# Attention block with residual on one core: first and last steps reordered on GpSimd and VectorE, and filler products on TensorE at the start

## The chip, the core and the metric

The kernel runs on one core of a Trainium2 chip. A core has five engines, each with its own instruction queue that it works through in order: TensorE (PE in the profile, its weight loads PEld), VectorE (DVE), ScalarE (ACT), GpSimd (POOL) and SyncE (SP, which here only issues DMAs). Engines wait for one another through semaphores. The metric is the device time of one execution in microseconds (us), as a median over runs.

## The reference

One layer of multi-query attention over 64 batches of 128 tokens with 512 features, 16 heads of width 64, added to its input. Cut to what matters:

```python
B, N, DIM, H, DH = 64, 128, 512, 16, 64
xn  = layernorm(x, g_in)                        # (x-mean)*rsqrt(var+1e-5)*g
q   = (xn @ Wq).reshape(B, N, H, DH).transpose(0, 2, 1, 3) * DH**-0.5
k, v = split(xn @ Wkv)                          # one key and value head for all 16
k   = concat([null_kv[0], k]); v = concat([null_kv[1], v])      # one null token
sim = einsum('bhid,bjd->bhij', q, k) + concat([null_attn_bias, attn_bias])
sim = where(causal, -max, sim); sim = where(mask, sim, -max)
out = einsum('bhij,bjd->bhid', softmax(sim), v)
x   = x + layernorm(out.reshape(B, N, H*DH) @ Wo, g_out)
```

All of it is fp32.

## The kernel before

**Tiles and stages.** Tokens are taken in rows of 128 (`m`), four rows to a group (`g`), 16 groups; a batch `b` is 128 tokens. For each batch the scores of all 16 heads, `S[b]`, lie in one SBUF tile of 128 x 16 x 129, of which column 128 is the null token. Three such tiles rotate (pool `sp`, three buffers, which the start also uses for `prod`). `S[b]` is first filled with bias plus mask (`bias_mask`, L370, POOL) and with the null column (L376, POOL). The scores are then added from PSUM in two halves of eight heads (L396, DVE), each followed by its negative maximum (L397, DVE). Sixteen exps run on ACT (L409) and leave their sums; the reciprocals come from DVE (L427), and POOL scales the weights by them (L432). DVE transposes 32 x 32 blocks (`blocks_T`, L448), ten DMAs on SP move the blocks into place (`blocks_move`, L459, tile `aTb`), PE multiplies by the values (`values`, L483), ACT copies the result out (L490), PE multiplies by `wo` (`out_mm`, L502). `out_stats` takes mean and variance (L509 to L513, DVE), the power -1/2 on POOL (L514), and centres and scales by `g_out` (L516, DVE). `residual` multiplies by the power on ACT (L530) and adds x on POOL (L531); `store` writes it.

**Token rows.** `norm_stats` (L197 to L201 on DVE, the power on POOL at L202) and `norm_apply` (nmr L214 on DVE, then L215 on ACT) normalise a row. Rows 0 to 7 are transposed on PE (`norm_T`, L224, and the copy L225 on ACT), later ones on DVE and by DMA. `kv_mm` makes key, value and null score (L256, then L264 to L269 on DVE), `k_T` transposes the key (L275, L277).

**Queries.** For group 0 they are plain products (`q_plain`, L294, copies L301). For the other groups one level of Strassen's scheme is used, seven products instead of eight per block (`product`, L337), with sums of the weights made once (`weight_sums`, L304 to L307, DVE, both inputs in SBUF) and sums of the tokens once per group (`token_sum`, L320, POOL). Partial products are copied out on ACT (`keep`, L348) and added on DVE (L355).

**Order.** The order on each engine is written out by hand: what `step(n)` issues first comes first. `step(n)` runs for n from -6 to 62 and works on many batches at once: token row n+10 or n+11 is normalised, keys and values of row n+6 are made, bias and mask of batch n+3 are put down, scores of batch n+2 are made, exps of batch n+1, values of batch n and the output of batch n-1. Steps up to n = 0 are the fill (`fill`), where the halves of the exps are spread out between the query products; from n = 58 on there are no queries left. PSUM is short: products of kv, transposes, values and output (`pw`, `pkv`, `pkT`, `po`, `py`) rotate through two buffers of pool `ps_w`, and the scores through two of `ps_s`.

Lines that set the order around the change:

```python
for m in mns:
    norm_stats(m)
...
if ok(n + 1) and fill:
    exps_half(n + 1, 1)        # exps, reciprocal (DVE), scale (POOL)
...
if ok(n + 2):
    scores(n + 2, 0)
    scores(n + 2, 1)
```

The functions that the diff touches:

Of the kernel before, what the change touches and what calls it, by code (L numbers as in the profile page):

```python
# [8 lines left out]
FP = mybir.dt.float32  # L9
# [8 lines left out]
def kernel(  # L18
# [45 lines left out]
    nc = tc.nc  # L64
# [152 lines left out]
    def norm_T(m):  # L217
        g, t = divmod(m, GB)
        if t == 0:
            xT[g] = gp.tile([P, KC, TOK], FP, tag="xT", name=f"xT_{g}")  # L220
        xh = xs.pop(m)
        pt = ps_w.tile([P, KC, P], FP, tag="w", name=f"pxT_{m}")
        for kc in range(KC):
            nc.tensor.transpose(pt[:, kc, :], xh[:, kc * P : (kc + 1) * P], ident)  # L224
        nc.scalar.copy(xT[g][:, :, t * N : (t + 1) * N], pt)  # L225
# [83 lines left out]
    def token_sum(g, k):  # L309

        xS[g, k] = gp.tile([P, HK, HT], FP, tag=f"xS{k}", name=f"xS{k}_{g}", bufs=1)
        b11, b12 = xT[g][:, lo_k, lo_t], xT[g][:, lo_k, hi_t]
        b21, b22 = xT[g][:, hi_k, lo_t], xT[g][:, hi_k, hi_t]
        p, m = {
            1: (b12, b11),
            2: (b22, xS.get((g, 1))),
            3: (b22, b12),
            4: (b21, xS.get((g, 2))),
        }[k]
        nc.gpsimd.tensor_tensor(xS[g, k], p, m, ALU.subtract)  # L320
# [39 lines left out]
    def mask_neg(g):  # L360
        mneg[g] = gp.tile([P, TOK], FP, tag="mneg", name=f"mneg_{g}")
        nc.vector.tensor_scalar(
            mneg[g], m8s.pop(g), 0.0, NEG, ALU.is_equal, ALU.mult
        )

    def bias_mask(b):
        g, t = divmod(b, GB)
        S[b] = sp.tile([P, 2, NC, N + 1], FP, tag="s", name=f"s_{b}")
        s = S[b].rearrange("p r c j -> p (r c) j")
        nc.gpsimd.tensor_tensor(  # L370
            s[:, :, 0:N],
            bflat,
            mneg[g][:, t * N : (t + 1) * N].unsqueeze(1).broadcast_to([P, H, N]),
            ALU.add,
        )
        nc.gpsimd.tensor_copy(s[:, :, N : N + 1], sn.pop(b).unsqueeze(2))  # L376

    def scores(b, hf):
# [38 lines left out]
    def exps_half(b, hf):  # L417
        exps(b, 8 * hf, 8 * hf + 8)
        rinv(b, hf)
        scale(b, hf)  # L420
# [23 lines left out]
    def blocks_T(b):  # L444

        s = S[b].rearrange("p r c j -> p (r c) j")
        sb = hp.tile([P, NQ, H, Q], FP, tag="sb", name=f"sb_{b}", bufs=1)
        nc.vector.transpose(  # L448
            sb.rearrange("p j h q -> p h j q"),
            s[:, :, 0:N].rearrange("p h (j k) -> p h j k", k=Q),  # L450
        )
        sbs[b] = sb
# [54 lines left out]
    def out_stats(b):  # L507
        st = small.tile([P, 6], FP, tag="st", name=f"sto_{b}")
        nc.vector.bn_stats(st, ys[b])  # L509
        mv = small.tile([P, 2], FP, tag="mvo", name=f"mvo_{b}")  # L510
        nc.vector.bn_aggr(mv, st)
        rstd = small.tile([P, 1], FP, tag="rstdo", name=f"rstdo_{b}")
        nc.vector.tensor_scalar(rstd, mv[:, 1:2], EPS, None, ALU.add)  # L513
        nc.gpsimd.tensor_tensor(rstd, rstd, nhalf, ALU.pow)  # L514
        y = hp.tile([P, DIM], FP, tag="y", name=f"y_{b}")
        nc.vector.scalar_tensor_tensor(  # L516
            y, ys.pop(b), mv[:, 0:1], gob, ALU.subtract, ALU.mult
        )
        if b == B - 1:

            nc.vector.scalar_tensor_tensor(y, y, rstd, res.pop(b), ALU.mult, ALU.add)
        else:
            yr[b] = y, rstd
        ys[b] = y
# [45 lines left out]
    def step(n):  # L570
        def ok(b, end=B):
            return 0 <= b < end

        qg, part = divmod(n + 6, GB)
        mT, mkv, mk = n + 10, n + 6, n + 5
        mns = [m for m in (n + 10, n + 11) if ok(m) and (m >= 2 * GB) == (m == n + 11)]
        if part == 0 and ok(qg + 1, NG) and n + 6 >= 0:
            load_mask(qg + 1)
        q, f = ok(qg, NG), part
        last_g, last_f = divmod(n + 5, GB)  # L580
        fast, last = q and qg > 0, 0 < last_g < NG


        fill = n <= 0
        if fast and f == 0 and fill:
            for k in range(1, 5):
                token_sum(qg, k)
        if ok(n + 3) and q:
            bias_mask(n + 3)
        for m in mns:  # L590
            norm_stats(m)
        if fast and f == 0 and not fill:
            token_sum(qg, 1)

        tT = ok(mT) and mT >= 2 * GB
        if tT and mT % GB:
            tokens_T(mT)
        moves = tT and (mT + 1) % GB == 0
        if moves:
            tokens_move(mT // GB)  # L600
        if ok(n + 1) and not fill:
            exps_half(n + 1, 0)
            exps_half(n + 1, 1)
        if tT and mT % GB == 0:
            tokens_T(mT)
        if ok(n + 3) and not q:
            bias_mask(n + 3)
        if ok(n - 1):
            out_mm(n - 1)
            out_stats(n - 1)  # L610
        if fast and f == 0 and not fill:
            for k in range(2, 5):
                token_sum(qg, k)
        if last:
            product(last_g, last_f, 4, ps_q, "a", start=False)
            q_out(last_g, HC + last_f, lo_t, "a")
            product(last_g, last_f, 3, ps_q, "c", start=False)
            q_out(last_g, last_f, hi_t, "c", "u2")
        if ok(n + 1) and fill:
            exps_half(n + 1, 0)  # L620
        for m in mns:
            norm_apply(m)
        if fast:
            if f == 0:
                qT[qg] = gp.tile([P, NC, TOK], FP, tag="qT", name=f"qT_{qg}")
            product(qg, f, 2, ps_w, "w")
            product(qg, f, 1, ps_q, "a")
            keep("a", "p1")
            q_out(qg, f, lo_t, "w", "p1")
            product(qg, f, 5, ps_q, "c")  # L630
        elif q:
            q_plain(qg, 2 * f)
        if ok(n + 1) and fill:
            exps_half(n + 1, 1)
        if ok(n - 1) and q:
            residual(n - 1)
        if ok(n + 2):
            scores(n + 2, 0)
            if not q and n + 1 < B - 2:
                blocks_T(n + 1)  # L640
            scores(n + 2, 1)
        if n == B - 2:
            attn_T_pe(n)
        if ok(n):
            values(n, 0)
            values(n, 1)
        if ok(n - 1) and not q:
            residual(n - 1)
        if n + 1 in sbs:
            blocks_move(n + 1)  # L650
        if fast:
            product(qg, f, 6, ps_q, "a", start=False)
            keep("a", "u2")
        elif q:
            q_plain(qg, 2 * f + 1)
        if mT < 2 * GB:
            norm_T(mT)
        if ok(mkv) and mkv >= GB - 1:
            kv_mm(mkv)


        if ok(n - 1):
            store(n - 1)
        if not moves:
            loads_late(n)
        if ok(n + 1) and q and not fill:
            blocks_T(n + 1)
            blocks_move(n + 1)
        if moves:
            loads_late(n)  # L670
        if fast:
            product(qg, f, 7, ps_q, "a", start=False)
            keep("a", "u3")
        if ok(mk) and mk >= GB - 2:
            k_T(mk)
        if fast:
            q_out(qg, HC + f, hi_t, "c", "u3")
        if ok(n + 1) and fill:
            blocks_T(n + 1)
            blocks_move(n + 1)  # L680
        if n == -4:
            for m in range(GB - 1):
                kv_mm(m)
                if m:
                    k_T(m - 1)
        if part == 2 and ok(qg, NG):
            mask_neg(qg)


    nc.vector.tensor_scalar(gin8, gin, DH**-0.5, None, ALU.mult)  # L690
# [7 lines left out]
    norm_stats(3)  # L698
    norm_apply(2)
    norm_T(2)  # L700
    norm_apply(3)
    norm_T(3)
    load_second()
    weights_q(2)
    weights_q(0)
# [6 lines left out]
    for n in range(-6, B - 1):  # L712
        step(n)
        if n == -6:
            for kc in range(2):
                weights_kv(kc)
            for kc in range(2, KC):
                weights_kv_prod(kc)
            load_late()
        if n == -5:  # L720
            for kc in range(2, KC):
                weights_kv(kc)
            nc.gpsimd.affine_select(
                bflat,
                bflat,
                pattern=[[0, H], [-1, N]],
                compare_op=ALU.is_ge,
                fill=NEG,
                base=0,
                channel_multiplier=1,  # L730
            )
            weight_sums()

    load_res(B - 1)
# [47 lines left out]
```

## Time and profile before

| | |
|---|---|
| median of 3 runs | 1229.79 us (1229.73 to 1230.2) |
| the profiled execution | 1230.63 us, of which its span, first to last instruction, 1228.5 us |
| TensorE | busy 1183.7 us (96%) |
| VectorE | busy 813.4 us (66%) |
| ScalarE | busy 679.0 us (55%) |
| GpSimd | busy 771.5 us (63%) |
| bias and mask sum, L370 on POOL | 64 of 4535 ns |
| scale, L432 on POOL | 128 of 1900 ns |
| exp, L409 on ACT | 1024 of 392 ns, overlapping with its accumulator read |
| score sum L396 and maximum L397 on DVE | 128 each, 1217 and 1228 ns |
| block transpose L448 on DVE | 62 of 2301 ns |
| mean granted TensorE clock | 0.991 |

A busy share is an average over the whole span. The profile also cuts the span into 40 equal slices of 30.7 us and gives each engine a digit for each (9 is 90% or more), and it lists the time an engine sat idle together with the engine and line whose result ended it. A wait for several semaphores is put down to the one that came last by the profile, which can be a coincidence. A start time and a duration stand ahead of each row of a timeline; the durations on one engine may overlap by about 0.1 us[...].

### The profile page before, as it was taken

How to read it: one execution, taken by the hardware profiler on the slowest of the kernel's cores; microseconds unless marked ns; L12 is line 12 of the kernel's file. 1: busy time of each engine (PE TensorE's matmuls, PEld its weight loads, DVE VectorE, ACT ScalarE, POOL GpSimd, SP SyncE). 2: the span in 40 equal slices, each digit the busy share in tenths (PEclk: the TensorE clock that was granted, in tenths of full speed). 3: DMA queues.
4: the chain of work that ended last, by engine and by line, in shares of the span. 5: the costliest groups of instructions: out<-in, count | busy, mean ns of one | idle time of the engine just before them, and what ended most of it. 6: DMA issues, size and time to landing. Idle time of an engine off the chain costs nothing.

```text
span 1228.5 us, 19153 instructions
## 1 busy us (share of the span) xinstructions
PE 1183.7 (96%) x5968; PEld 750.8 (61%) x5968; DVE 813.4 (66%) x1491; ACT 679.0 (55%) x2563; POOL 771.5 (63%) x520
## 2 busy tenths in 40 slices
PE   5968999999999999999999999999999999999987
PEld 2555666666666666666666666666666666666443
DVE  6565776677677667667767767766776776666652
ACT  3244655665665565566556556556655655554662
POOL 5345747657674765767576585766658576665651
PEclk9979999999999999999999999999999999999999
DMA  6203324333342433334243333434333342322231
GB/s 199 98 14 81 109 78 101 95 101 102 85 113 79 105 96 97 102 83 112 83 106 92 95 100 86 109 85 103 97 89 99 93 105 81 91 70 73 67 88 43
DMA packets 96883, 113.81 MB, mean 93 GB/s; under 512 B 17424, under 2 KB 50704, under 8 KB 96784
## 3 DMA queue, kind: packets, MB, share of 16 engines
q1 hardware_dynamic: 95968, 111.55, 33.2%
q8 instruction: 48, 0.79, 0.3%
q10 hardware_dynamic: 816, 1.05, 0.2%
q14 instruction: 51, 0.42, 0.1%
HBM read 40.45 MB, written 16.78 MB: 47 GB/s over the span
## 4 chain that ended last, share of the span: by engine, by line
PE 87%; ACT 2%; DVE 2%; POOL 2%; issue 1%; SPq 1%; DMA 0%; DVEq 0%; ACTq 0%; POOLq 0%
PE py L502 34%; PE pa L337 17%; PE ps L386 9%; PE po L483 9%; PE pc L337 8%; PE pkv L256 5%; PE pw L337 4%; ACT s L409 2%; POOL s L370 1%; PE pkT L275 1%; SPq L459 0%; DVE s L396 0%; DMA res<-in_x_dram 0%; DVE sb L448 0%; DVE nmax L397 0%
## 5 line engine op out<-in xcount | busy, mean ns | idle before, releaser
L370 POOL TENSOR_TENSOR s<-biasc,mneg 128x2048 f32<-128x2048 f32 x64 | 290.2, 4535 | 332.3 <-DVE sb L448 214.0
L502 PE MATMUL py<-wo,oT 128*128 128x512 f32 x1024 | 453.6, 596 | 5.6 <-ACT oT L490 2.9
L409 ACT ACTIVATE s<-s,nmax 128x129 f32<-128x129 f32 x1024 | 396.2, 392 | 0.0
L502 PEld LDWEIGHTS py<-wo,oT 128*128 128x128 f32 x1024 | 190.8, 191 | 230.5 <-issue 219.7
L432 POOL TENSOR_TENSOR s<-s,rinv 128x1024 f32<-128x1024 f32 x128 | 240.6, 1900 | 30.9 <-DVE rinv L427 27.9
L396 DVE TENSOR_TENSOR s<-ps,s 128x1024 f32<-128x1024 f32 x128 | 155.8, 1217 | 61.0 <-PE ps L386 61.0
L409 ACT ACTIVATION_READ_ACCUMULATOR s<-s,nmax 128x1 f32 x1024 | 194.6, 190 | 0.0
L397 DVE TENSOR_REDUCE nmax<-s 128x8 f32<-128x1032 f32 x128 | 157.2, 1228 | 4.6
L490 ACT ACTIVATE oT<-po,nv 128x512 f32<-128x512 f32 x128 | 87.9, 687 | 122.3 <-PE po L483 122.0
L427 DVE RECIPROCAL rinv<-rsum 128x8 f32<-128x8 f32 x128 | 24.1, 189 | 182.1 <-ACT s L409 182.1
L448 DVE STREAM_TRANSPOSE sb<-s 128x2048 f32<-128x2048 f32 x62 | 142.7, 2301 | 0.3 <-issue 0.3
L337 PE MATMUL pa<-xS,wS 128*128 128x256 f32 x480 | 131.4, 397 | 7.6 <-ACT kp L348 6.7
L386 PEld LDWEIGHTS ps<-kT,qT 64*128 64x128 f32 x2048 | 119.3, 188 | 22.5 <-issue 21.7
L386 PE MATMUL ps<-kT,qT 64*128 64x128 f32 x2048 | 131.5, 278 | 0.0
L483 PE MATMUL po<-aTb,v 128*64 128x512 f32 x512 | 125.3, 605 | 4.9 <-DMA res<-in_x_dram 1.9
L337 PEld LDWEIGHTS pa<-xS,wS 128*128 128x128 f32 x480 | 83.2, 192 | 61.8 <-ACT oT L490 34.9
L531 POOL TENSOR_TENSOR y<-y,res 128x512 f32<-128x512 f32 x63 | 80.3, 1275 | 46.3 <-ACT y L530 46.3
L348 ACT COPY ku<-pa 128x256 f32<-128x256 f32 x120 | 44.7, 372 | 116.0 <-PE pa L337 116.0
L215 ACT ACTIVATE x<-x,nmr,rstd 128x512 f32<-128x512 f32 x60 | 48.7, 813 | 100.6 <-DVE nmr L214 79.7
L355 DVE TENSOR_TENSOR qT<-pw,kp 128x256 f32<-128x256 f32 x60 | 25.5, 425 | 91.1 <-ACT kp L348 91.1
L530 ACT ACTIVATE y<-y,rstdo 128x512 f32<-128x512 f32 x63 | 45.5, 722 | 71.0 <-POOL rstdo L514 62.7
L256 PE MATMUL pkv<-wkv,xT 128*128 128x144 f32 x512 | 74.3, 289 | 0.9 <-DVE sn L269 0.6
(71 smaller groups left out, 1338.5 us busy)
## 6 DMA issues: line engine op xcount, KB each, us to landing
aTb<-sb SPq DMA_DIRECT2D x620, 64.0 KB
x<-in_x_dram SPq DMA_DIRECT2D x64, 256.0 KB
res<-in_x_dram SPq DMA_DIRECT2D x64, 256.0 KB
out_dram<-y SPq DMA_DIRECT2D x64, 256.0 KB
xT<-xb SPq DMA_DIRECT2D x224, 64.0 KB
wo<-in_L_cond_Wo_dram SPq DMA_DIRECT2D x1, 2048.0 KB
wq<-in_L_cond_Wq_dram ACTq DMA_DIRECT2D x2, 512.0 KB
wq<-in_L_cond_Wq_dram SPq DMA_DIRECT2D x2, 512.0 KB
```

The lines of the kernel that those rows point to most:

```text
L256: nc.tensor.matmul(pkv, xT[g][:, kc, t * N : (t + 1) * N], wkv[:, kc, :], start=(kc == 0), stop=(kc == KC - 1),)
L337: nc.tensor.matmul(prod[tag], w[:, kc, f * P : (f + 1) * P], t[:, kc, :], start=(start and kc == 0), stop=(kc == HK - 1), skip_group_check ...
L370: nc.gpsimd.tensor_tensor(s[:, :, 0:N], bflat, mneg[g][:, t * N : (t + 1) * N].unsqueeze(1).broadcast_to([P, H, N]), ALU.add,)
L386: nc.tensor.matmul(ps[:, r, c, :], qT[g][rows, hf * HC + c, toks], kT[b][rows, :], start=True, stop=True,)
L396: nc.vector.tensor_tensor(sv, ps, sv, ALU.add)
L397: nc.vector.tensor_reduce(nmax[b][:, :, cs], S[b][:, :, cs, :], AX.X, ALU.max, negate=True)
L409: nc.scalar.activation(S[b][:, r, c, :], S[b][:, r, c, :], AF.Exp, bias=nmax[b][:, r, c : c + 1], accum_out=rsum[b][:, r, c : c + 1],)
L432: nc.gpsimd.tensor_tensor(sv, sv, rinvs.pop((b, hf)).unsqueeze(3).broadcast_to([P, 2, HC, N]), ALU.mult,)
L448: nc.vector.transpose(sb.rearrange("p j h q -> p h j q"), s[:, :, 0:N].rearrange("p h (j k) -> p h j k", k=Q),)
L483: nc.tensor.matmul(po[r * DH : (r + 1) * DH], v[b], aTb[:, 2 * hf : 2 * hf + 2, r], start=True, stop=True,)
L490: nc.scalar.activation(oT[b][:, :, hf * 2 * Q : (hf + 1) * 2 * Q].rearrange("p c (i q) -> p i c q", q=Q), po, AF.Identity, bias=nv2,)
L502: nc.tensor.matmul(py, oT[b][:, c, :], wo[:, c, :], start=(c == 0), stop=(c == NC - 1))
```

## The change

`bias_mask` is split into `bias_add` (the sum L370) and `null_copy` (the null column). The bias sums of batches 0, 1 and 2 move from steps -3, -2 and -1 to the end of step -5 and into steps -4 and -3; `mask_neg(0)` goes with the first of them, ahead of the weight sums. In step -2 the four token sums move behind `norm_stats`. In every later step with queries the null column moves behind `norm_stats` and, where there is one, behind the first token sum. In steps -1 and 0 the second reciprocal and scale go between the two score halves. In steps 58 to 60 the bias sum goes behind `out_mm` and `out_stats`, whose power is thereby ahead of it on POOL. At the start, 8 and then 10 products of the identity with itself are put on TensorE, around the transposes of token row 3; their result is not read.

```diff
-    def bias_mask(b):
+    def bias_add(b):
         g, t = divmod(b, GB)
         S[b] = sp.tile([P, 2, NC, N + 1], FP, tag="s", name=f"s_{b}")
         s = S[b].rearrange("p r c j -> p (r c) j")
...
             ALU.add,
         )
+
+    def null_copy(b):
+        s = S[b].rearrange("p r c j -> p (r c) j")
         nc.gpsimd.tensor_copy(s[:, :, N : N + 1], sn.pop(b).unsqueeze(2))
...
         fill = n <= 0
-        if fast and f == 0 and fill:
-            for k in range(1, 5):
-                token_sum(qg, k)
-        if ok(n + 3) and q:
-            bias_mask(n + 3)
+        early = n + 3 < 3
+        if ok(n + 3) and q and not early:
+            bias_add(n + 3)
         for m in mns:
             norm_stats(m)
-        if fast and f == 0 and not fill:
+        if fast and f == 0:
             token_sum(qg, 1)
+            if fill:
+                for k in range(2, 5):
+                    token_sum(qg, k)
+        if 1 <= n + 5 < 3:
+            bias_add(n + 5)
+        if ok(n + 3) and q:
+            null_copy(n + 3)
...
-        if ok(n + 3) and not q:
-            bias_mask(n + 3)
         if ok(n - 1):
             out_mm(n - 1)
             out_stats(n - 1)
+        if ok(n + 3) and not q:
+            bias_add(n + 3)
+            null_copy(n + 3)
...
         if ok(n + 1) and fill:
-            exps_half(n + 1, 1)
+            exps(n + 1, 8, 16)
...
             scores(n + 2, 0)
             if not q and n + 1 < B - 2:
                 blocks_T(n + 1)
+            if ok(n + 1) and fill:
+                rinv(n + 1, 1)
+                scale(n + 1, 1)
             scores(n + 2, 1)
...
-        if part == 2 and ok(qg, NG):
+        if part == 2 and 0 < qg < NG:
             mask_neg(qg)
+
+    def keep_busy(k):
+
+        pb = ps_s.tile([P, P], FP, tag="s", name="busy")
+        for _ in range(k):
+            nc.tensor.matmul(pb, ident, ident, start=True, stop=True)
...
     norm_T(2)
+    keep_busy(8)
     norm_apply(3)
     norm_T(3)
+    keep_busy(10)
     load_second()
...
                 channel_multiplier=1,
             )
+            mask_neg(0)
+            bias_add(0)
             weight_sums()
```

## The prediction

> **What bounds the kernel now.** I read the slices first, then a table of stages cut where TensorE starts and stops waiting, then TensorE's waits, then each engine's timeline at both ends.
>
> ```profile
> PE   5968999999999999999999999999999999999987
> ...
> PEclk9979999999999999999999999999999999999999
> ```
>
> ```profile
> 60.33:67.08 6.75, 0.00 (x1) 0.04 (x1) 0.33 (x2) 1.07 (x2) 6.75 (x5) 0.66 0.08 30
> ...
> 114.64:1136.75 1022.11, 1022.11 (x5286) 661.91 (x5285) 701.48 (x1293) 590.93 (x2242) 669.07 (x447) 1.00 0.35 94
> ```
>
> The columns of a stage are its length, then busy time of PE, PEld, DVE, ACT, POOL, then clock, DMA share, GB/s. From 114.64 to 1136.75 us PE is busy for the whole 1022.11 us at full clock, so nothing the other engines do faster there moves the end. What can be won lies in the first 115 us and the last 92.
>
> ```profile
> PE pa L337 <- ACT kp L348: 6.7, 1, 6.7
> ...
> PE pc L337 <- DVE qT L355: 2.9, 1, 2.9
> PE py L502 <- DVE sn L269: 2.7, 1, 2.7
> ```
>
> These are the three long waits of the fill (total, times, longest, us). The first is explained by POOL's and ACT's timelines (start, duration):
>
> ```profile
> 60.39 4.50 POOL L370 TENSOR_TENSOR s<-biasc,mneg 128x2048 f32<-128x2048 f32 x1
> 64.83 0.21 POOL L376 COPY s<-sn 128x16 f32<-128x16 f32 x1
> 64.98 0.55 POOL L202 TENSOR_TENSOR rstd<-rstd,nhalf 128x1 f32<-128x1 f32 x1
> ```
>
> ```profile
> 65.86 0.81 ACT L215 ACTIVATE x<-x,nmr,rstd 128x512 f32<-128x512 f32 x1 [10.58 <-issue]
> 66.58 0.35 ACT L348 COPY kp<-pa 128x256 f32<-128x256 f32 x1
> ```
>
> POOL works in order: the bias sum of batch 1 stands ahead of the power that token row 9 needs; ACT's normalisation of it stands ahead of the copy kp, and PE's next product waits for kp. One-microsecond stages show what this does to the clock: 0.50 from 62.5 to 72.7, 89.8 to 93.2 and 106.9 to 110.3, each after a stretch of about 3.4 us in which PE was less than half busy.
>
> At the end the same shape returns three times:
>
> ```profile
> 1174.20 4.53 POOL L370 TENSOR_TENSOR s<-biasc,mneg 128x2048 f32<-128x2048 f32 x1
> 1178.67 0.21 POOL L376 COPY s<-sn 128x16 f32<-128x16 f32 x1
> 1178.83 0.55 POOL L514 TENSOR_TENSOR rstdo<-rstdo,nhalf 128x1 f32<-128x1 f32 x1
> ```
>
> ```profile
> 1179.41 0.72 ACT L530 ACTIVATE y<-y,rstdo 128x512 f32<-128x512 f32 x1 [3.64 <-POOL rstdo L514]
> 1180.04 0.39 ACT L409 ACTIVATE s<-s,nmax 128x129 f32<-128x129 f32 x1
> ```
>
> The 16 exps (6.2 us) queue behind y, y behind the power, the power behind the bias.
>
> **The change part by part, on PE's time.**
>
> 1. Busy matmuls. A 512-column pass took 0.855 us at first (weight loads at 19.18, 20.04, 20.89) and 0.43 us from 21.65, though the clock row prints 1.00. So 128 columns cost 0.214 cold, 0.107 warm; a full fp32 product is two passes; 18 of them cost 7.7 us cold. Warm, the q products would save some 2 us, but they start later: the first 8 hold x 3's transposes from 14.5 to about 16.4, the other 10 end at 19.7 (clock up near 18) to 21.5 (not up), and 16 passes of 0.43 then end between 26.6 and 28.4, against 26.4. Neither matters: PE's next hard point is x 6's transposes at 41.01, which wait for DVE, POOL and ACT. If that chain stays as it is, this part costs 0 to 1.6 us; if it gets later, nothing.
>
> 2. Bias sum 0 and the mask before the weight sums. The mask row (0.41) now precedes them on DVE, so x 6's statistics are at least 0.41 late. Bias sum 0 waits for the mask, at about 33.9, when POOL is idle (from 30.5 to 39.3): it meets the four weight sums (33.35 to 38.2 before; 1.22 us each).
>
> ```profile
> 24.42 2.44 POOL L552 TENSOR_TENSOR prod<-wq,nkb 128x1024 f32<-128x1024 f32 x1 [1.38 <-DVE nq L564]
> ```
>
> ```profile
> 25.81 1.08 DVE L565 COPY wkv<-nq 128x16 f32<-128x16 f32 x1
> ...
> 33.26 0.17 DVE L565 COPY wkv<-nq 128x16 f32<-128x16 f32 x1
> 33.35 1.22 DVE L304 TENSOR_TENSOR wS<-wq 128x1024 f32<-128x1024 f32 x1
> ```
>
> A DVE copy that meets POOL's product ends only when POOL ends (26.9): 1.08 us instead of 0.17. The score sums L396, also tensor-tensor, keep 1.2 us beside POOL, but one of their inputs is in PSUM. No row shows a DVE sum with both inputs in SBUF beside POOL, which the weight sums are. Bounds: 0 (as L396) and all of bias sum 0, 4.5 us (as L565); a gain is excluded. The Trainium skill, "SBUF — State Buffer", section "Who interferes with whom", speaks against the change: a DVE instruction with two SBUF inputs contends with a POOL instruction that reads SBUF, and one blocks for the other's whole length. By L396 the transposes of x 6 come at 41.4; by the page, the first weight sum runs, bias sum 0 takes 34.9 to 39.4, the other three end at 43.1, then statistics, power, nmr, ACT (2.8 us before) give 45.9. I take the page: +4.9. PE then idles 4.6 us, enough for one or two half-clock stretches of 3.4 us over some 4 us of work: +1.3 to +2.7, I take +2.0.
>
> 3. Bias sums 1 and 2 early. Each goes to POOL a step or two sooner, behind powers 6 and 8, where DVE has only PSUM reads and small operations. Power 7 no longer waits for bias sum 0: the waits of 0.6 (x 7) and 0.5 (its copy) go, -1.1. Token sums now stand behind power 9, which waits for DVE: pc waits for the first of them, +1.4 (58.1 where PE came at 56.7, on the scale without part 2).
>
> 4. From there, by the same scale. Power 9 ends at 56.8, x 9 at 57.9, kp at 58.2: PE never waits for kp. Scores of batch 0 reach DVE at 60.1 instead of 67.3. Then exps, the reciprocal, scale and transposes follow with the durations of the rows. PE's eight waits from 60.33 to 105.84 were 6.75, 0.38, 0.90, 0.41, 2.89, 1.44, 0.35, 2.69 = 15.8. Mine after: 0.25 and 1.0 (qT of step -1), 0.45, 1.15 (qT of step 0), 1.6 (the same, second half), 1.95 (aTb's DMAs, 7.9 us after the transposes as before), 0.35, 0.45 = 7.2. So -8.6.
>
> 5. Reciprocals between score halves (two steps). In step 0 the reciprocal waited on DVE for the exps and held two score sums and two maxima (4.8 us) back; one pair (2.4 us) now goes ahead. It is inside those 7.2: without it 1.15 and 0.45 would each be about 2.4 longer. The scale on POOL comes no later, since the reciprocal is still ready only when ACT ends. What is queued behind it is the second score half, as before.
>
> 6. Half clock. 62.5 to 72.7 cost 2.8 us of work after 67.1, the other two stretches 1.7 each: -6.2. After, no stretch of 3.4 us has over half idle, the nearest 45%; one that still trips costs 1.7.
>
> 7. Null column behind the power and a token sum, in all steps to 57: POOL's sum is unchanged. Every fourth step the copy now also stands behind the wait of the first token sum for its 16 transfers; but the scale already did, and the 0.21 us copy is read by a maximum two steps later. SP's and ACT's orders are the same throughout. PE has no wait there: 0.
>
> 8. Power ahead of bias, steps 58 to 60. Walked with the durations above: y of step 58 goes 0.75 earlier; in 59 ACT's exps end at 1169.05 instead of 1171.9; in 60 this matters for PE:
>
> ```profile
> 1173.15 0.74 DVE L516 SCALAR_TENSOR_TENSOR y<-py,mvo,gob 128x512 f32<-128x512 f32 x1
> ```
>
> ```profile
> 1173.95 1.08 PE L483 MATMUL po<-aTb,v 128*64 128x512 f32 x4 [1.90 <-DMA res<-in_x_dram]
> ```
>
> The second half of the values takes the PSUM slot that L516 reads, and starts when L516 ends (1173.89); the printed DMA is a coincidence. L516 stands behind the reciprocal behind the exps. It now ends at 1171.05: the 1.90 goes, hence also the half clock after it (py 8.53 instead of 7.1), of step 61's 0.88 some 0.3 stays (there the DMAs of aTb come last), and the 1.69 before the last transposes stays. Bias sums 61 to 63 begin at 1146.2, 1159.8, 1171.8, not later than 0.6 us after before, and are read 8 us later. Sum -4.7, lower bound -3 (if the clock still drops).
>
> Total: +4.9 +2.0 -1.1 +1.4 -8.6 -6.2 -4.7 = -12.3. The span goes from 1228.5 to 1216.2; with the 2.1 us outside it 1218.3 against the profiled run's 1230.63. That run is 0.84 above the median 1229.79, so 1217.5.
>
> **The rivals.**
>
> No contention (part 2 costs 0.41 and no clock): 0.41 -1.1 +1.4 -8.6 -6.2 -4.7 = -18.8, 1211. For it: tensor-tensor rows beside POOL keep their time. Against: the page, and L565.
>
> The fill gives nothing. Contention as above, PE held at half clock through steps -3 to 0 (each stretch there has a gap), which would take back its 7.6 us, so that the tail alone is left (1225), or 2 to 3 more (1228). Against: the 6.9 us of q products in step -3 have no gap, and such a stretch brought the clock up at 21.6 and 72.7.
>
> Slower. Only part 7 acts some sixty times. If null copy behind power and token sum held up the scale, and that PE, it would have to cost 12.3/58 = 0.21 us a step to cancel the gain, 0.26 to be slower by 0.2%; at 0.3 a step, 1235. Against: PE's gap-free 1022 us, and everything that stood ahead of the scale still does.
>
> That the change doesn't do what it says: the bias sums do move on POOL; the busy matmuls may leave the clock down. Priced in part 1.
>
> **How the numbers follow.** Contention 0.60, with a range of its own of 1214.5 (no clock loss, tail full) to 1221 (both stretches, tail at -3). No contention 0.28: 1209 to 1213.5. Nothing from the fill 0.06, split over same and faster. Slower 0.06. The 8-in-10 range is 1209.5 to 1221.5. 0.2% (2.5 us) is about what a measurement of this kernel can tell from no change. Faster 0.90, same 0.04, slower 0.06.
>
> **What would show it.** Right: PE's 6.7 us on kp gone; three rows L370 ahead of the first token sum; a weight sum of some 5.7 us or a bias sum of more than 5 between 33 and 44 us, and x 6's transposes near 46; clock low once near 45 to 52 instead of at 62 to 73; y of step 60 ahead of its bias sum and no 8.5 us py. Weight sums at 1.22 us and transposes at 41.4 would show the first rival. A PE wait in the steady steps would make all of it wrong.

## The result and the profile after

The changed kernel takes 1218.99 us (1217.28 to 1220.67, 4 runs), the kernel before beside it 1229.76 us (1229.63 to 1230.2): a ratio of 0.99, 95% interval [0.9887, 0.9913]. It is faster by 10.8 us; 12.3 was forecast. The profiled execution took 1219.43 us with a span of 1217.3. In the changed kernel the lines are numbered 3 higher from the exps on (score sum L399, reciprocal L430, scale L435, values L486, y's product L505), and bias sum and null copy are L370 and L379.

The slices, which look the same but for the start:

```profile
PE   6789999999999999999999999999999999999997
...
PEclk9899999999999999999999999999999999999999
```

TensorE's waits from 10 to 115 us (total, times, longest):

```profile
PE pxT L224 <- ACT x L215: 6.2, 1, 6.2
PE po L486 <- DMA aTb<-sb: 2.6, 1, 2.6
...
PE pc L337 <- DVE qT L355: 2.2, 3, 1.3
PE pc L337 <- POOL xS L320: 1.1, 1, 1.1
```

The 6.7 us on kp is gone, and so are 2.9 on qT and 2.7 on sn. In their place stands one new wait of 6.2 us, for token row 6. DVE's and POOL's timelines (start, duration) tell where it is from:

```profile
33.55 1.22 DVE L304 TENSOR_TENSOR wS<-wq 128x1024 f32<-128x1024 f32 x1
34.69 5.54 DVE L305 TENSOR_TENSOR wS<-wq 128x1024 f32<-128x1024 f32 x1
40.26 1.23 DVE L306 TENSOR_TENSOR wS<-wS,wq 128x1024 f32<-128x1024 f32 x1
```

```profile
33.78 5.36 POOL L370 TENSOR_TENSOR s<-biasc,mneg 128x2048 f32<-128x2048 f32 x1 [3.42 <-DVE mneg L362]
```

Bias sum 0 started beside the first weight sum. The second weight sum ended 1.09 us after the bias sum (40.23 against 39.14), that is, it took about its own 1.22 us once POOL was done. The statistics of row 6 stand behind the fourth. On TensorE's timeline:

```profile
45.53 1.12 PE L224 MATMUL pxT<-ident,x 128*128 128x128 f32 x4 [6.17 <-ACT x L215]
...
64.59 1.13 PE L337 MATMUL pc<-xS,wS 128*128 128x256 f32 x4 [1.08 <-POOL xS L320]
...
94.76 1.10 PE L486 MATMUL po<-aTb,v 128*64 128x512 f32 x4 [2.59 <-DMA aTb<-sb]
```

Row 6's transposes began at 45.53 us; the forecast was 45.9. Stages cut at the clock's edges (length, busy time of PE, PEld, DVE, ACT, POOL, then clock, DMA share, GB/s):

```profile
41.03:44.44 3.41, 0.00 (x0) 0.00 (x0) 2.64 (x6) 0.00 (x0) 0.60 (x2) 1.00 0.00 0
44.44:51.27 6.83, 5.26 (x22) 4.87 (x22) 1.40 (x8) 2.35 (x4) 4.43 (x1) 0.50 0.11 35
...
92.00:95.50 3.50, 0.91 (x6) 0.23 (x4) 2.78 (x3) 3.50 (x18) 1.19 (x1) 1.00 0.44 112
95.50:99.00 3.50, 3.50 (x12) 2.86 (x11) 2.52 (x3) 1.65 (x5) 1.90 (x1) 0.53 0.27 95
107.35:1129.46 1022.11, 1022.11 (x5287) 661.91 (x5285) 701.53 (x1293) 590.76 (x2242) 671.10 (x450) 1.00 0.35 95
```

Both times the clock falls behind a stretch of about 3.41 us in which PE was little busy: not at all in the first, 26% in the second. The second fall, at 95.5, was not forecast. The steady part, from the end of batch 0's output product (107.35 us; 114.64 before) to the start of batch 57's, is 1022.11 us as before; it starts 7.29 us earlier. At the end, the product of step 60 and POOL's order:

```profile
1166.41 7.13 PE L505 MATMUL py<-wo,oT 128*128 128x512 f32 x16 [0.79 <-ACT oT L493]
```

```profile
1164.24 0.55 POOL L517 TENSOR_TENSOR rstdo<-rstdo,nhalf 128x1 f32<-128x1 f32 x1
1164.76 4.54 POOL L370 TENSOR_TENSOR s<-biasc,mneg 128x2048 f32<-128x2048 f32 x1
```

The power now stands ahead of the bias sum; the 1.90 us wait and the product of 8.53 us are gone. From the start of batch 57's product to the end it is 87.84 us instead of 91.75: 3.9 less. Fill 7.3 and tail 3.9 make the 11.2 by which the span is shorter.

### The profile page after: what moved, and what is told of

It reads as the page before. It is cut to its first block, busy times and chain, and to the rows that moved or that the text cites. A ratio compares the mean times of both kernels' runs of the same rounds, so it can differ in the third digit from the quotient of the medians.

```text
span 1217.3 us, 19225 instructions
## 1 busy us (share of the span) xinstructions
PE 1181.3 (97%) x6004; PEld 753.9 (62%) x6004; DVE 817.4 (67%) x1491; ACT 678.8 (56%) x2563; POOL 772.0 (63%) x520
## 4 chain that ended last, share of the span: by engine, by line
PE 91%; DVE 1%; ACT 1%; SPq 0%; issue 0%; DMA 0%; DVEq 0%
PE py L505 36%; PE pa L337 17%; PE ps L389 10%; PE po L486 10%; PE pc L337 8%; PE pkv L256 5%; PE pw L337 4%; PE pkT L275 1%; SPq L462 0%; ACT s L412 0%; DVE aTb L476 0%; ACT oT L493 0%; DVE sb L451 0%; DMA aTb<-sb 0%; PE paT L472 0%
## 5 line engine op out<-in xcount | busy, mean ns | idle before, releaser
L370 POOL TENSOR_TENSOR s<-biasc,mneg 128x2048 f32<-128x2048 f32 x64 | 291.1, 4549 | 324.3 <-DVE sb L451 209.5
L505 PE MATMUL py<-wo,oT 128*128 128x512 f32 x1024 | 450.4, 593 | 2.9 <-ACT oT L493 2.9
L505 PEld LDWEIGHTS py<-wo,oT 128*128 128x128 f32 x1024 | 189.6, 190 | 225.6 <-issue 214.8
L435 POOL TENSOR_TENSOR s<-s,rinv 128x1024 f32<-128x1024 f32 x128 | 240.5, 1899 | 27.0 <-DVE rinv L430 25.4
L399 DVE TENSOR_TENSOR s<-ps,s 128x1024 f32<-128x1024 f32 x128 | 155.9, 1218 | 62.9 <-PE ps L389 62.9
L430 DVE RECIPROCAL rinv<-rsum 128x8 f32<-128x8 f32 x128 | 24.2, 189 | 173.4 <-ACT s L412 173.4
L486 PE MATMUL po<-aTb,v 128*64 128x512 f32 x512 | 125.1, 605 | 3.8 <-DMA aTb<-sb 2.6
L256 PEld LDWEIGHTS pkv<-wkv,xT 128*128 128x128 f32 x512 | 73.8, 197 | 4.1 <-PE pkT L275 0.9
```

Source lines behind the costliest of these rows:

```text
L256: nc.tensor.matmul(pkv, xT[g][:, kc, t * N : (t + 1) * N], wkv[:, kc, :], start=(kc == 0), stop=(kc == KC - 1),)
L370: nc.gpsimd.tensor_tensor(s[:, :, 0:N], bflat, mneg[g][:, t * N : (t + 1) * N].unsqueeze(1).broadcast_to([P, H, N]), ALU.add,)
L399: nc.vector.tensor_tensor(sv, ps, sv, ALU.add)
L435: nc.gpsimd.tensor_tensor(sv, sv, rinvs.pop((b, hf)).unsqueeze(3).broadcast_to([P, 2, HC, N]), ALU.mult,)
L486: nc.tensor.matmul(po[r * DH : (r + 1) * DH], v[b], aTb[:, 2 * hf : 2 * hf + 2, r], start=True, stop=True,)
L505: nc.tensor.matmul(py, oT[b][:, c, :], wo[:, c, :], start=(c == 0), stop=(c == NC - 1))
```

## The experiments

Twelve kernels ran, four to a chip (two of the twelve are the changed kernel itself), with nine runs of the kernel before beside each four (medians 1230.83, 1230.63 and 1230.46 us). Times below are medians; a ratio is to those runs.

**1. Is it the two inputs?** In `e1_one_input` the four weight sums become block transposes of nearly the same length that read one operand; the kernel leaves out the sums.

```diff
-        nc.vector.tensor_tensor(s3, a11, a21, ALU.subtract)
-        nc.vector.tensor_tensor(s1, a21, a22, ALU.add)
...
+        nc.vector.transpose(s3, a11)
+        nc.vector.transpose(s1, a21)
```

> The changed kernel with the four weight sums replaced by four block transposes of the same 1024 elements, which have one SBUF input instead of two (the query products of groups 1 to 15 are therefore made from other weights). Contention (one input less, no lock): no row of these lines is longer than 1.3 us, bias sum 0 takes 4.5 us, row 6's transposes start near 41.4 us instead of 45.5, no half clock between 45 and 50 us, and the time falls from 1219.0 to between 1211 and 1214. Rival, that the order alone (mask ahead of the sums, bias sum ahead of power 6) makes row 6 late: it stays at 45 us or later and the time stays within 1217 to 1221.

Measured: 1212.43 us (1212.18 to 1214.31), ratio 0.9854 [0.9839, 0.9869]. That is the expected time. The bias sum lies over the same four instructions, at the same place, and on the two timelines neither is stretched:

```profile
34.40 1.20 DVE L305 STREAM_TRANSPOSE wS<-wq 128x1024 f32<-128x1024 f32 x1
```

```profile
33.47 4.54 POOL L370 TENSOR_TENSOR s<-biasc,mneg 128x2048 f32<-128x2048 f32 x1 [3.42 <-DVE mneg L362]
```

PE starts row 6 at 40.76. So it is not the order alone (the mask is still ahead of these instructions, the bias sum still in the same place). The kind of instruction changed with the number of inputs, but the score sums L399 are sums of two operands too, one of them in PSUM, and the 56 of them that run beside a POOL instruction of over 1 us in the changed kernel's profile take 1.23 us at most. That leaves the second input read from SBUF, as the Trainium skill has it ("SBUF — State Buffer", "Who interferes with whom"). One input from SBUF is not safe in itself: the small copy in the prediction's part 2 reads one, and took 1.08 us instead of 0.17 beside POOL.

**2. The same cause taken away without leaving anything out.** In `e2_bias_later` mask and bias sum 0 go to step -4, behind the weight sums and row 6's power, and bias sums 1 and 2 one step later than in the change:

```diff
-        if 1 <= n + 5 < 3:
-            bias_add(n + 5)
+        if n + 4 == 0:
+            mask_neg(0)
+        if 0 <= n + 4 < 3:
+            bias_add(n + 4)
...
-            mask_neg(0)
-            bias_add(0)
```

> The changed kernel with the mask row and bias sums 0, 1 and 2 one step later each: bias sum 0 behind power 6 in step -4, 1 behind powers 7 and 8 in step -3, 2 behind the token sums in step -2, so that POOL is idle during the weight sums. Contention: weight sums 1.22 us each, row 6's transposes near 41.0 us, time 1210.5 to 1213.5. Rival, that early bias sums are what the fill needs and later ones hold up the scores of batches 0 to 2: 1216 or more.

Measured: 1212.76 us (1212.35 to 1214.41), ratio 0.9854 [0.9841, 0.9868]. That is the expected time. TensorE waits 0.15 us for row 6 instead of 6.17, and later waits are those of the change, 7 us earlier:

```profile
40.67 0.66 PE L224 MATMUL pxT<-ident,x 128*128 128x128 f32 x4 [0.15 <-ACT x L215]
...
57.39 1.13 PE L337 MATMUL pc<-xS,wS 128*128 128x256 f32 x4 [1.08 <-POOL xS L320]
...
87.55 1.38 PE L486 MATMUL po<-aTb,v 128*64 128x512 f32 x4 [2.57 <-DMA aTb<-sb]
```

With 1 this gives the contention a price: about 6 us of the changed kernel's time (the differences of the ratios to 0.99 and 0.9908 are 5.7 to 6.6 us). Bias sum 0 need not be that early: nothing in the fill came later for it.

**3. The tail by itself.** `e3_tail_only` is the kernel before with part 8 alone:

```diff
-        if ok(n + 3) and not q:
-            bias_mask(n + 3)
         if ok(n - 1):
             out_mm(n - 1)
             out_stats(n - 1)
+        if ok(n + 3) and not q:
+            bias_mask(n + 3)
```

> The kernel before with only the last part of the change (steps 58 to 60: power ahead of bias). By the traces the last stage (from PE's product py of step 58 to the end) shrank from 91.75 to 87.84 us: 1225.9, range 1225 to 1226.8. Rival, that part of the tail's gain came from the fill's shift of clock windows: 1227 to 1228.5.

Measured: 1225.5 us (1224.73 to 1225.98), ratio 0.9954 [0.9942, 0.9967], as expected. The interval makes 4 to 7 us; its profiled tail is 87.35 us, 4.4 less than before. So the tail is 35 to 40% of the gain by the profiles (3.9 or 4.4 of 11.2), and adds to the rest.

**4. The busy matmuls.** `e4_no_busy` and `e4b_no_busy` are one kernel, the change without the 18 of them, run on two chips; on the second the changed kernel itself ran beside it as `a3_after_again`.

```diff
-    keep_busy(8)
...
-    keep_busy(10)
```

> The changed kernel without the 18 busy products. PE waits 6.2 us for row 6 in any case, so by the prediction's part 1 they matter nothing: 1218 to 1220, query products of 0.855 us per pass at first and a shorter wait for row 6. Rival, that they settle the clock later in the fill too: a half-clock stretch more and 1220.5 to 1223.

> The changed kernel without the 18 busy products once more, now beside the changed kernel on one chip. Theory (the busy products only bring PE sooner to the wait of token row 6, make its gap 2 us longer and so the half clock behind it more likely): 2 to 2.5 us less than the changed kernel, 1216 to 1217. Rival (prediction, part 1: nothing either way, and the earlier difference was the chip's): within 0.7 us of the changed kernel.

> The changed kernel unaltered, as the reference for the three kernels beside it on the same chip: 1217 to 1221 us, ratio 0.99. Its own runs are spread over 3 us; the theory for that is that the half-clock stretches come at a moment that is not tied to the program, so the profile shows one or two of them, and the first product of batch 0's outputs starts between 97.5 and 100.5 us.

Measured: 1216.45 us (1216.07 to 1217.79), ratio 0.9884 [0.987, 0.9897]; then 1217.91 (1217.18 to 1219.12), ratio 0.9897 [0.9883, 0.991], beside 1220.23 (1216.46 to 1220.59), ratio 0.9908 [0.9893, 0.9924]. The first lies below both of the times expected for it, the second 2.3 us below the changed kernel beside it, where the rival had 0.7 at most. The intervals overlap, so the medians alone do not decide. What the busy matmuls do is seen in TensorE's timelines, of the changed kernel

```profile
12.79 2.42 PE L705 MATMUL busy<-ident 128*128 128x128 f32 x16
...
17.72 7.03 PE L294 MATMUL pq<-xT,wq 128*128 128x512 f32 x16
```

and of the one without (`e4b_no_busy`):

```profile
17.25 9.82 PE L294 MATMUL pq<-xT,wq 128*128 128x512 f32 x16 [1.72 <-ACT wq L547]
...
45.59 0.66 PE L224 MATMUL pxT<-ident,x 128*128 128x128 f32 x4 [3.91 <-ACT x L215]
```

They do bring the clock up: the first q products take 7.03 us instead of 9.82. But row 6 is ready at about 45.5 either way, so PE only waits longer: 6.17 us instead of 3.91. The longer gap cost two half-clock stretches where 3.91 cost one: from row 6's transposes to the k,v product behind them (51.18 and 50.33) it is 5.65 us against 4.74, 0.9 more. The other difference is the wait for aTb, 2.59 us against 1.75, 0.8 more. Together they are the 1.7 us by which batch 0's output product starts earlier (98.61 against 100.32). One pair of profiles could be chance, but the others agree. All five with the busy matmuls in which row 6 is late have two stretches there, the two without have one; the way to the k,v product is 5.64 or 5.65 us in four of the five (4.89 in `a2_after_again`), against 4.74 and 4.92. The wait for aTb is 2.1 to 2.6 us in the changed kernel's three profiles and `e9_null_back`, against 1.74 and 1.75. Of the ten DMA issues for aTb on SP (shortest, median, longest in ns) one takes 1.4 us with the busy matmuls,

```profile
L462 SPq DMA_DIRECT2D aTb<-sb x10: 576/588/1416, 86.1 to 92.7; - x10
```

and none does without (`e4b_no_busy`):

```profile
L462 SPq DMA_DIRECT2D aTb<-sb x10: 576/588/622, 85.2 to 90.9; - x10
```

The last section returns to it.

**5. The reciprocal.** `e5_rinv_back` puts the second reciprocal and scale of the fill back ahead of both score halves; `a2_after_again` is the changed kernel on that chip.

```diff
-            exps(n + 1, 8, 16)
+            exps_half(n + 1, 1)
...
-            if ok(n + 1) and fill:
-                rinv(n + 1, 1)
-                scale(n + 1, 1)
```

> The changed kernel with one part undone: in the steps of the fill the second reciprocal and its scale stand again ahead of both score halves. The prediction (part 5) says that without the move the waits of 1.15 and 0.45 us in step 0 would each be about 2.4 us longer: +4.8 us against the changed kernel, or +2.3 if only the first of the two counts in the end; so 1221 to 1224. The rival: step 0 is set by the DMAs of aTb and by the half clock, and the order on DVE is hidden by them: +0, within 1 us of the changed kernel.

> The changed kernel once more, unaltered, as the reference on this chip. By what it ran before: 1217 to 1221 us, 0.99 of the kernel before. The first row of the transposes of token row 6 at 45.5 us after a wait of about 6, half clock once near 45 to 52 us and once near 95 to 99.

Measured: 1222.4 us (1221.93 to 1223.09), ratio 0.9932 [0.9919, 0.9944], beside 1219.06 (1217.3 to 1220.22), ratio 0.9902 [0.9888, 0.9916]: the move is worth 3.3 us, within the 1221 to 1224 expected. The two waits that were named, on qT and on sn, grew (waits from 5 to 112 us; 1.3 and 0.3 at the longest in `a2_after_again`), by less than the 2.4 each that was said, and that for aTb shrank from 2.1 to 1.5:

```profile
PE pc L337 <- DVE qT L355: 3.4, 2, 2.9
PE py L505 <- DVE sn L269: 2.1, 1, 2.1
PE po L486 <- DMA aTb<-sb: 1.5, 1, 1.5
```

The clock is at half behind the wait of 2.9, from 85.1 to 91.9 us, where it is not in `a2_after_again`, so a part of the 3.3 us is clock.

**6. The null column.** `e9_null_back` copies it directly behind the bias sum again, from batch 3 on:

```diff
         if ok(n + 3) and q and not early:
             bias_add(n + 3)
+            null_copy(n + 3)
...
-        if ok(n + 3) and q:
+        if ok(n + 3) and q and early:
             null_copy(n + 3)
```

> The changed kernel with one part undone: in the steps from batch 3 on, the null column is again copied directly after the bias sum, ahead of the power and the first token sum; in the fill the order of the change stays. Prediction, part 7: 0, within 0.5 us of the changed kernel, and the same 1022 us from the second batch's to the 58th's output product. Rival: the order is worth 0.05 us a step in one direction or the other, 3 us.

Measured: 1219.25 us (1218.41 to 1219.47), ratio 0.9905 [0.9892, 0.9919], beside 0.9908 for the changed kernel (`a3_after_again`). In both profiles it is 1011.08 us from the start of batch 1's output product to the start of batch 57's (118.32 to 1129.40, and 117.65 to 1128.73).

**7. What is left of the fill.** `e6_later_no_busy` is `e2_bias_later` without the busy matmuls. `e7_gaps_filled` is `e2_bias_later` with two gaps filled:

```diff
+        if fast and f == 0 and fill:
+            token_sum(qg, 1)
         for m in mns:
             norm_stats(m)
...
-        if ok(n):
+        if ok(n) and n > 0:
             values(n, 0)
             values(n, 1)
...
             product(qg, f, 6, ps_q, "a", start=False)
             keep("a", "u2")
+            if n == 0:
+                values(n, 0)
+                values(n, 1)
```

`e8_gaps_no_busy` is that without the busy matmuls.

> The kernel e2_bias_later (first bias sum behind the weight sums) without the 18 busy products. Theory: once token row 6 is not held up, PE's arrival decides; without busy products PE comes to its transposes at 41.4 us instead of 40.5, so this costs about +0.7 to +1: 1213 to 1214, ratio 0.986. Rival (the busy products only cost, as e4 hints by 2.5 us in the changed kernel): 1210 to 1212, ratio 0.984 or less.

> The kernel e2_bias_later with two of its remaining PE gaps filled: in step -2 the first token sum goes to POOL ahead of the power that it stood behind (wait of 1.1 us for it), and in step 0 one product (1 us of work) goes ahead of the values that wait 2.6 us for the DMAs of aTb. Theory: the first 1.1 us is taken off, and the gap of 2.6 becomes 1.5, so the half clock behind it (about 1.5 us) does not come: 1.5 to 3.5 us less than e2, ratio 0.9825 to 0.984, 1209 to 1211 us. Rival: the end of the fill is set by the chain of batch 0 over exps, scale and aTb, so PE waits later by what it saved before: within 0.5 us of e2.

> The kernel e7_gaps_filled without the 18 busy products. Where e7 runs, no half clock is left behind the fill's gaps, so by the theory that busy products hurt through the half clock alone they have nothing left to cost, and their 0.7 to 1 us of earlier arrival stays: e8 equal to e7 or up to 1 us slower, 1210.5 to 1211.5, ratio 0.9836 to 0.9845. Rival (they cost 2 us whatever follows): 1208.5, ratio 0.982.

Measured: e6 1210.95 us (1210.39 to 1212.37), ratio 0.9841 [0.9828, 0.9855]; e7 1210.55 (1209.39 to 1212.66), 0.9836 [0.9821, 0.9851]; e8 1209.07 (1208.73 to 1209.61), 0.9824 [0.9811, 0.9838]. For e6 the rival's range came, so the theory that the busy matmuls help there failed; e7 lies where its theory put it, e8 between its two. The profiles of e6, e7 and e8 show no half-clock stretch in the fill; e2 still has one behind its wait of 2.57 us. In e6 PE waits 1.75 for aTb:

```profile
87.05 1.08 PE L486 MATMUL po<-aTb,v 128*64 128x512 f32 x4 [1.75 <-DMA aTb<-sb]
```

In e6 none of aTb's ten issues is long, in e2 one is 1.40 us; that is the shorter wait, and behind it the clock stayed up. In e7, PE does not wait for aTb at all, but 1.43 for kp:

```profile
84.22 1.13 PE L337 MATMUL pa<-xS,wS 128*128 128x256 f32 x4 [1.43 <-ACT kp L348]
85.28 2.30 PE L486 MATMUL po<-aTb,v 128*64 128x512 f32 x8
```

```profile
77.78 4.52 POOL L370 TENSOR_TENSOR s<-biasc,mneg 128x2048 f32<-128x2048 f32 x1 [3.61 <-DVE sb L451]
82.25 0.56 POOL L202 TENSOR_TENSOR rstd<-rstd,nhalf 128x1 f32<-128x1 f32 x1
```

This is once more the shape that the change took away elsewhere: the bias sum of batch 3, which was not moved, stands ahead of the power, ACT's normalisation (83.09) waits for the power, and kp (83.81) stands behind that.

The gain of e7 over e2 is about 2 us by the ratios, with intervals that overlap. e8 against e7 gives no clear answer (1.5 us less by medians, on two chips; the profiled spans are 1207.5 and 1207.4): whether busy matmuls cost anything where PE does not wait for aTb was not settled. e8 is the fastest here, 11.2 us below the changed kernel on its chip (`a3_after_again`), and the intervals are far apart.

## Why the prediction was right, point by point

The likeliest case came: contention as the page has it, and most of the fill's other waits gone. The fill came out at -7.3 us by the profile; -7.6 was forecast. Between common points of the two PE timelines:

- Part 2, delay: row 6 from 41.01 to 45.53, +4.5 (forecast +4.9). The rule, not the row L396, gave the size; experiment 1 shows why L396 was no guide.
- Part 2, clock: from row 6 to the next k,v product 5.65 us instead of 3.38, +2.3 (+2.0).
- Part 3: from there to the first scores 14.48 us instead of 13.88, +0.6 (+0.3). The wait for the first token sum was 1.08, not 1.4; a new one of 0.58 on sn took the place of one that went.
- Part 4: after the scores, PE's waits are 0.45, 0.47, 0.16, 0.41, 0.49, 1.27 and 2.59 = 5.8 against 15.8 before, -10.0 (-8.6). aTb was undersized, 1.95 for 2.59, by the one long DMA issue of experiment 4; the others were oversized.
- Part 6: this failed in part. "No stretch of 3.4 us has over half idle" was wrong, and could have been seen to be: its own wait of 1.95 us is 57% of 3.41. The stretch from 92.0 to 95.5 was 26% busy and the next ran at half clock. So of the forecast -6.2, one of the three stretches came back (about 1.7): from the first scores to the end of batch 0's output product, waits taken off, PE needed 35.85 us instead of 40.56, -4.7.
- Parts 4 and 6 were off by 1.4 and 1.5 us in opposite directions; the good sum owes something to that.
- Part 1: the clock came up near 14 us (16 busy passes in 2.42 us, where 0.214 us each would be 3.42 cold and 0.107 each 1.71 warm), not at 18 to 21.5, so PE arrived at 39.4 instead of 41.3 and waited 6.2 instead of 4.6. The trace's first clock record is of this rise, at 13.8 us (21.5 before); for the time ahead of it a row prints 1.00 for want of a record. The claim "if it gets later, nothing" left out that a longer gap costs clock: 0.9 us by the pair of profiles in experiment 4, and 0.8 more by way of the DMA issue, which nothing in the profile of before showed.
- Part 5: +3.3 us without it (experiment 5), where two waits of 2.4 more had been named. They grew by 1.6 and 1.8.
- Part 7: 0, as said (experiment 6).
- Part 8: -3.9 in the changed kernel, -4.4 alone (-4.7). The rows that the prediction named add up to 1.90 + 1.40 + 0.58 = 3.9; for the other 0.8 it named none. The wait ahead of step 61's values kept 0.48 us instead of 0.3.

The rivals: no contention did not happen, but experiments 1 and 2 made it happen, and it gives 1212.4 to 1212.8 where 1211 was worked out. That the fill gives nothing is refuted by the 7.3 us; that part 7 costs 0.21 us a step by 1011.08 against 1011.08.

## What to carry to other kernels

Before moving a long GpSimd instruction, look what VectorE does at its new place: a sum of two operands in SBUF took 5.54 us instead of 1.22 beside one. Price an idle gap of TensorE with the clock behind it, and measure the gap against 3.4 us, not against the work; work that only brings TensorE sooner to a wait can cost. Where two terms of a sum rest on the same waits, check one against the other.

## What had not been expected

**Where the 3.4 us stretches lie is not tied to the program.** In each trace the clock's edges lie whole multiples of 3.41 us apart, but the first, at which it rises, comes at 13.8, 14.6 and 15.8 us in the changed kernel's three profiles, and in the fill it then falls once or twice. In `a2_after_again` the clock fell from 41.86 to 48.68 us and not again, although PE waited 2.13 for aTb; in the first profile it fell at 44.44 and again at 95.5. Batch 0's output product starts at 97.81 in the one and at 100.32 in the other, and 2.1 us lie between their times (1217.3 and 1219.43). Likewise `e4b_no_busy` lost the clock behind the same wait of 1.75 us that `e6_later_no_busy` had without loss. The Trainium skill says that the window is free-running ("TensorE: Matmul & The Clock Gate", Part 1), and these edges agree. On one chip the changed kernel's five runs (`a3_after_again`) are spread over 4.1 us, and the four of e8, whose profile has no fall in the fill, over 0.9; that the falls make the spread is likely, not shown.

This grid, carried on from a trace's own edges, gives the busy share at which the clock turns. The stretch before a loss in `e4b_no_busy`:

```profile
90.97:94.38 3.41, 1.66 (x8) 0.57 (x7) 2.69 (x3) 3.41 (x17) 1.30 (x1) 1.00 0.56 134
```

and one without a loss in `a2_after_again`:

```profile
89.63:93.04 3.41, 1.57 (x15) 0.57 (x12) 1.65 (x3) 2.54 (x11) 2.59 (x4) 1.00 0.39 93
```

PE was 49% busy in the one and 46% in the other. All 14 traces, cut on this grid up to 1198 us, narrow it down. At full clock each of the 19 stretches in which PE was under 41% busy was followed by half clock, and none of the 4791 above 50%; of the six between 44 and 50%, only that of `e4b_no_busy`. At half clock the ten stretches with PE up to 71% busy left it there, and the 20 from 83% on brought it back. So here the clock falls below about 40 to 50% busy and needs over 71% to return; modelled ends and missing records may blur this by a few per cent.

**A DMA issue on SP became longer where only TensorE's stream had changed.** In all eight profiles of kernels with the busy matmuls one of aTb's ten issues in step 0 took 0.97 to 1.65 us; in all six without, the kernel before among them, none took over 0.63. The DMA traffic of the microsecond in which that issue begins, 90 to 91 us of the changed kernel (packets, MB, share of the 16 engines), holds one packet of the queue that loads instructions:

```profile
q8 instruction: 1, 0.02, 7.7%
```

It is there likewise at 89 in `a2_after_again` and at 83 in `e1_one_input` and `e2_bias_later`, and absent from the issues of `e4b_no_busy`, where such packets come at 75 and 99 us. In each of the eight one such packet of 16 KB begins just before the long issue, and in none of the six does one come during the ten. Over the whole of the 14 traces, 163 of 8680 issues for aTb took more than 0.8 us, and 153 of these overlap such a packet in time; of the 8517 shorter ones 221 do. So long issues and these loads go together. That the load makes the issue longer, and that 72 more TensorE instructions moved its moment, is still argued: no run took it away by itself.

**A blocked VectorE instruction shows as a long one, not as a wait.** L305 is listed as 5.54 us of busy time, so VectorE's busy share tells nothing of it; only its mean beside the same instruction elsewhere (1.22 us) does. POOL's side is stretched too, from 4.54 to 5.36: by 0.82 us, most of the 0.99 for which the first weight sum still ran when the bias sum began (33.78 to 34.77).
